# Pairwise products of each row: who issues the stores

## The chip, the cores and the metric

The kernel runs on one core of one Trainium2 chip. The metric is the device time of one execution in microseconds (us); the time of a version is the median of its runs. Beside it stands the span of a profiled execution, which is a little shorter because it leaves out what lies before the first and after the last recorded instruction.

A core has several engines that work side by side, each with its own list of instructions: VectorE (DVE in the profile), ScalarE (ACT), GpSimd (POOL), SyncE (SP) and TensorE (PE, not used here). Data move between the off-chip memory and the on-chip memory through 16 DMA engines. An engine starts such a transfer by an instruction in its own list; the letter q after an engine's name in the profile marks that side of it (SPq).

## The reference

For each of 4096 rows of 256 numbers, all products of two elements of the row are wanted, each pair once: the upper triangle of the outer product, 256 x 257 / 2 = 32896 numbers.

```python
# inputs: r_inputs, 4096 x 256, float32
dot = jnp.einsum('bi,bj->bij', inputs, inputs)
iu, ju = jnp.triu_indices(d)          # d = 256
return dot[:, iu, ju]                 # 4096 x 32896, float32
```

The input has 4.19 MB, the output 538.97 MB. There are two operations in the whole kernel that matter: the multiplication, and the writing of the output.

## The kernel before

Partition p of the on-chip memory holds the rows 32p to 32p + 31. The work is cut into 16 groups of two rows per partition (REPEAT = 2), and each group into 5 pieces of the output's columns (PIECES = 5), so there are 80 tiles. A tile has 128 partitions x 2 rows x up to 6592 columns of float32 and lies in one of three buffers that are used in turn.

```python
P = 128
UNIT = 64
REPEAT = 2
PIECES = 5
BUDGET = 0.95
FIRST = [512, 1536, 3584]
...
    xpool = ctx.enter_context(tc.tile_pool(name="x", bufs=1))
    opool = ctx.enter_context(tc.tile_pool(name="o", bufs=3))

    x_in = x.rearrange("(p r) d -> p (r d)", p=P)
    x_out = out.rearrange("(p g r) c -> g p r c", p=P, r=REPEAT)
```

The whole input is loaded once, in three transfers (of 256, 1792 and 2048 KB) that SyncE issues:

```python
    cuts = [0, REPEAT * d, total // 2, total]
    for a, b in zip(cuts, cuts[1:]):
        nc.sync.dma_start(xt[:, a:b], x_in[:, a:b])
```

Each tile is then computed and stored. ScalarE takes the first runs of columns of a block, VectorE the rest; a run is one element of the row times a stretch of the row. The two rows of a tile are stored by one transfer each (line 139 of the kernel), 128 rows of up to 26368 contiguous bytes. The very first tile is stored in four blocks, so that its first stores can start early.

```python
    for g in range(groups):
        for c, (lo, hi) in enumerate(zip(borders, borders[1:])):
            o = opool.tile([P, REPEAT, slot], F32, tag="o", name=f"o_{g}_{c}")
            first = g == c == 0
            cuts = [lo, *(FIRST if first else []), hi]
            for a, b in zip(cuts, cuts[1:]):
                block = runs(d, a, b)
                k = split(block, 0.0 if first else BUDGET * REPEAT * (b - a))
                for i, j, at, length in block[:k]:
                    ...
                        nc.scalar.activation(...)          # line 123
                ...
                for (i, j, at, length), m in interleave(block[k:]):
                    ...
                    nc.vector.tensor_tensor(...)           # line 132
                for r in range(REPEAT):
                    nc.sync.dma_start(x_out[g][:, r, a:b], o[:, r, a - lo : b - lo])   # line 139
```

That makes 79 x 2 + 4 x 2 = 166 stores. The framework puts in the semaphore waits: a store waits until VectorE and ScalarE have written its block, and the computation of a tile waits until the stores of the tile three back have landed.

Of the kernel before, what the change touches and what calls it, by code (L numbers as in the profile page):

```python
# [1 line left out]

# [4 lines left out]

F32 = mybir.dt.float32
AF = mybir.ActivationFunctionType
ALU = mybir.AluOpType  # L10
# [9 lines that stand above are left out]
def even_borders(lo: int, hi: int, pieces: int) -> list[int]:  # L20
    units = (hi - lo) // UNIT
    return [lo + units * c // pieces * UNIT for c in range(pieces)] + [hi]


def runs(d: int, lo: int, hi: int) -> list:


    found, at = [], 0
    for i in range(d):
        a, b = max(at, lo), min(at + d - i, hi)  # L30
        if a < b:
            found.append((i, i + a - at, a, b - a))
        at += d - i
    return found


def vector_ops(block: list) -> list:

    ops, k = [], 0
    while k < len(block):
        i, j, at, n = block[k]
        m = 2 if k + 2 < len(block) and i == j else 1
        ops.append((block[k], m))
        k += m
    return ops


def interleave(block: list) -> list:


    half = len(block)
    while half and len(vector_ops(block[:half])) > len(vector_ops(block[half:])):
        half -= 1
    a, b = vector_ops(block[:half]), vector_ops(block[half:])
    return [op for k in range(max(len(a), len(b))) for ops in (a, b) for op in ops[k : k + 1]]


def vector_time(block: list) -> float:
    return sum(68 + 1.046 * REPEAT * n * m for (*_, n), m in vector_ops(block))


def split(block: list, budget: float) -> int:


    scalar, k = 0.0, 0
    while k < len(block):
        scalar += REPEAT * (184 + 0.837 * block[k][3])  # L70
        if vector_time(block[k:]) <= budget or scalar > vector_time(block[k + 1 :]):
            break
        k += 1
    return k


def window(ap: bass.AP, free: list) -> bass.AP:
    return bass.AP(ap.tensor, ap.offset, [list(ap.ap[0]), *free])


@with_exitstack
def kernel(
    ctx: ExitStack, tc: tile.TileContext, x: bass.AP, out: bass.AP
):

    nc = tc.nc  # L90
    n, d = x.shape
    width = out.shape[1]
    assert n % (P * REPEAT) == 0 and width == d * (d + 1) // 2 and width % UNIT == 0
    groups = n // (P * REPEAT)
    borders = even_borders(0, width, PIECES)
    slot = max(b - a for a, b in zip(borders, borders[1:]))
# [8 lines that stand above are left out]
    total = n // P * d  # L105
    xt = xpool.tile([P, total + 1], F32, name="x")
    nc.vector.memset(xt[:, total:], 0.0)  # L107
# [14 lines that stand above are left out]
                        row = (g * REPEAT + r) * d  # L122
                        nc.scalar.activation(  # L123
                            o[:, r, at - lo : at - lo + length],
                            xt[:, row + j : row + j + length],
                            AF.Copy,
                            scale=xt[:, row + i : row + i + 1],
                        )
                row = g * REPEAT * d
                for (i, j, at, length), m in interleave(block[k:]):  # L130
                    at -= lo
                    nc.vector.tensor_tensor(  # L132
                        o[:, :, at : at + m * length],
                        window(xt[:, row + j :], [[d, REPEAT], [1, m], [1, length]]),
                        window(xt[:, row + i :], [[d, REPEAT], [1, m], [0, length]]),
                        ALU.mult,
                    )
                for r in range(REPEAT):
                    nc.sync.dma_start(x_out[g][:, r, a:b], o[:, r, a - lo : b - lo])  # L139


# [1 line left out]
_INS = ["r_inputs"]  # L143
_OUTS = [((4096, 32896), "float32")]


# [20 lines left out]
```

## Time and profile before

| what | value |
|---|---|
| time, median of 3 runs | 1274.17 us (1274.16 to 1274.32) |
| span of the profiled execution | 1272.5 us |
| VectorE busy, instructions | 996.1 us, 1813 |
| ScalarE busy, instructions | 486.7 us, 1547 |
| GpSimd busy, instructions | 0.2 us, 4 |
| moved by DMA | 543.43 MB |
| stores of a full row, time from issue to landing | 27.2 us (median of those of 3296 KB) |

How to read it: an engine's busy time is the sum of its instructions' durations; the instructions that only start a transfer or wait are not in it. The page also gives rows of 40 digits, the busy share of 40 equal slices of the span in tenths, and for each DMA queue the number of packets, the megabytes and the share of 16 engines' span that its packets took. A packet is one piece of a transfer on one DMA engine. A line of the timeline gives start, duration, engine, source line, operation, output and input shapes and count, and in brackets how long the engine had been idle before and what ended the idle time.

### The profile page before, as it was taken

The numbers are of one execution on the slowest core, as the hardware profiler recorded it, in microseconds if no ns is written. First come the engines' busy times: TensorE is split into PE (matmuls) and PEld (weight loads), VectorE is DVE, ScalarE is ACT, GpSimd is POOL, SyncE is SP. The second block draws the span as 40 slices with busy tenths as digits, with TensorE's granted clock in tenths as the row PEclk, the third lists the DMA queues.
The fourth block names the chain that finished last, engine by engine and source line by source line (L and its number), as shares of the span: only waits on it lengthen the run. The fifth ranks groups of instructions, "written<-read, shape, count | busy, mean of one in ns | idle before, by whom it ended". The sixth has DMA issues, their size and how long they took to land.

```text
span 1272.5 us, 3975 instructions
## 1 busy us (share of the span) xinstructions
DVE 996.1 (78%) x1813; ACT 486.7 (38%) x1547; POOL 0.2 (0%) x4
## 2 busy tenths in 40 slices
DVE  8987887878777787777877777777777777777770
ACT  5523535234342433424334252342523425234250
POOL 0000000000000000000000000000000000000000
DMA  9999999999999999999999999999999999999998
GB/s 384 435 433 430 434 433 427 434 432 427 431 428 432 429 430 431 429 431 429 433 427 431 429 431 429 431 430 430 429 432 427 433 427 432 428 432 429 431 427 346
DMA packets 24367, 543.43 MB, mean 427 GB/s; under 512 B 2704, under 2 KB 2704, under 8 KB 3344
## 3 DMA queue, kind: packets, MB, share of 16 engines
q1 hardware_dynamic: 24336, 543.17, 99.8%
q14 instruction: 31, 0.25, 0.0%
HBM read 4.19 MB, written 538.97 MB: 427 GB/s over the span
## 4 chain that ended last, share of the span: by engine, by line
DMA 70%; DVE 25%; issue 1%; SPq 1%; DVEq 0%
DMA out_dram<-o 70%; DVE o L132 25%; SPq L139 1%; DMA x<-in_r_inputs_dram 1%; DVEq L132 0%; SPq L110 0%
## 5 line engine op out<-in xcount | busy, mean ns | idle before, releaser
L132 DVE TENSOR_TENSOR o<-x 128x356 f32<-128x356 f32 (+61 forms) x1812 | 996.1, 634 | 239.9 <-DMA out_dram<-o 191.1
L123 ACT ACTIVATE o<-x 128x253 f32<-128x253 f32 (+41 forms) x1546 | 485.4, 404 | 748.6 <-DMA out_dram<-o 732.8
L123 ACT ACT_TABLE_LOAD x1 | 1.3, 1283 | 0.7 <-PEq L154 0.7
L107 DVE MEMSET x<- 128x1 f32 x1 | 0.1, 59 | 0.8 <-PEq L154 0.8
L154 POOL MEMSET const-uint8-127<- 128x1 uint8 x1 | 0.1, 102 | 0.0
L154 POOL MEMSET const-bfloat16-1.0<- 128x1 bf16 x1 | 0.1, 101 | 0.0
L154 POOL MEMSET const-float32-0.0<- 128x1 f32 x1 | 0.1, 98 | 0.2 <-issue 0.2
L154 POOL MEMSET const-float32-1.0<- 128x1 f32 x1 | 0.1, 98 | 0.0
## 6 DMA issues: line engine op xcount, KB each, us to landing
out_dram<-o SPq DMA_DIRECT2D x128, 3296.0 KB, 27.2
out_dram<-o SPq DMA_DIRECT2D x30, 3264.0 KB, 28.9
out_dram<-o SPq DMA_DIRECT2D x2, 1472.0 KB, 13.3
x<-in_r_inputs_dram SPq DMA_DIRECT2D x1, 2048.0 KB, 12.3
out_dram<-o SPq DMA_DIRECT2D x2, 1024.0 KB, 10.0
x<-in_r_inputs_dram SPq DMA_DIRECT2D x1, 1792.0 KB, 6.8
out_dram<-o SPq DMA_DIRECT2D x2, 512.0 KB, 10.2
out_dram<-o SPq DMA_DIRECT2D x2, 256.0 KB, 10.0
```

What stands on the lines that cost most here:

```text
L107: nc.vector.memset(xt[:, total:], 0.0)
L123: nc.scalar.activation(o[:, r, at - lo : at - lo + length], xt[:, row + j : row + j + length], AF.Copy, scale=xt[:, row + i : row + i + 1],)
L132: nc.vector.tensor_tensor(o[:, :, at : at + m * length], window(xt[:, row + j :], [[d, REPEAT], [1, m], [1, length]]), window(xt[:, row + ...
L139: nc.sync.dma_start(x_out[g][:, r, a:b], o[:, r, a - lo : b - lo])
L154: nc = _bacc.Bacc("TRN2", target_bir_lowering=False, num_devices=1)
```

## The change

The stores are issued by GpSimd in place of SyncE. [...] The computation, the tiles, the buffers and the transfers' shapes stay as they are, and so do the three loads, which SyncE still issues. The purpose is to have the stores on an engine that has nothing else to do, with a queue of their own.

```diff
@@ -136,7 +136,7 @@
                         ALU.mult,
                     )
                 for r in range(REPEAT):
-                    nc.sync.dma_start(x_out[g][:, r, a:b], o[:, r, a - lo : b - lo])
+                    nc.gpsimd.dma_start(x_out[g][:, r, a:b], o[:, r, a - lo : b - lo])
```

## The prediction, made before the changed kernel had run

> **What bounds the kernel now.** I read the utilisation rows of the page first, then its DMA queues, then the timeline of the steady part with the idle times in it, then the issues of the stores, and last the records of single DMA packets and landings.
>
> ```profile
> span 1272.5 us, 3975 instructions
> DVE 996.1 (78%) x1813; ACT 486.7 (38%) x1547; POOL 0.2 (0%) x4
> DMA  9999999999999999999999999999999999999998
> GB/s 384 435 433 430 434 433 427 434 432 427 431 428 432 429 430 431 429 431 429 433 427 431 429 431 429 431 430 430 429 432 427 433 427 432 428 432 429 431 427 346
> ...
> q1 hardware_dynamic: 24336, 543.17, 99.8%
> ...
> HBM read 4.19 MB, written 538.97 MB: 427 GB/s over the span
> ```
>
> The DMA row is full in every slice but the last, and the rate is flat at about 430 GB/s. The one queue of the kernel's transfers covers 99.8% of 16 engines' span. VectorE is busy 78% of the time and GpSimd does nothing after four memsets. This is a kernel limited by the transfer of its output.
>
> The timeline of a steady stretch shows how much slack stands behind that:
>
> ```profile
> 611.30 12.48 DVE L132 TENSOR_TENSOR o<-x 128x1008 f32<-128x1008 f32 x13 [3.15 <-DMA out_dram<-o]
> ...
> 626.98 12.37 DVE L132 TENSOR_TENSOR o<-x 128x896 f32<-128x896 f32 x14 [3.20 <-DMA out_dram<-o]
> 642.61 12.42 DVE L132 TENSOR_TENSOR o<-x 128x768 f32<-128x768 f32 x17 [3.26 <-issue]
> ...
> 658.21 12.38 DVE L132 TENSOR_TENSOR o<-x 128x612 f32<-128x612 f32 x21 [3.17 <-DMA out_dram<-o]
> ...
> 673.91 6.35 ACT L123 ACTIVATE o<-x 128x37 f32<-128x37 f32 x23 [9.95 <-DMA out_dram<-o]
> 673.93 6.32 DVE L132 TENSOR_TENSOR o<-x 128x372 f32<-128x372 f32 x19 [3.34 <-DMA out_dram<-o]
> ```
>
> Five tiles begin between 611.30 and 673.93, so one tile takes 62.63 / 4 = 15.66 us. VectorE needs 12.4 us of it and then waits 3.2 us for a buffer. A tile is two DMAs of 3296 KB, 6.75 MB, and 6.75 MB in 15.66 us is 431 GB/s, the rate of the page. There are three buffers. When VectorE starts a tile, the stores of the tile three back have just landed, and two tiles' stores are queued, 2 x 15.66 = 31.3 us of transfer. After 12.4 us, when it issues the new stores, 31.3 - 12.4 = 18.9 us are still ahead of them. The issues of line 139 confirm this:
>
> ```profile
> L139 SPq DMA_DIRECT2D out_dram<-o x166: 332/380/1227, 4.8 to 1237.4; - x166
> ...
> DMA to landing us min/median/max: 9.0/27.1/34.9
> ```
>
> The first store of a pair should land 18.9 + 7.8 = 26.7 us after its issue and the second 18.9 + 15.7 = 34.6 us after; the median is 27.1 and the maximum 34.9. SyncE spends 0.38 us on an issue. So a store may become ready up to about 18.6 us later than now (three buffers give 3 x 15.66 = 47.0 us a round, less 12.4 of VectorE, less 15.7 of its own transfer, less 0.3 of semaphores) before an engine runs dry.
>
> The packet records say what the transfer itself consists of. 24336 packets in 169 DMAs (166 stores and 3 loads) are 144 each, that is 16 engines x (8 rows + 1 semaphore write). A row of 26368 B goes as one packet: 16384 of them have a median of 980 ns, a mean of 983. Shorter ones take 84 ns (2048 B), 159 (4096 B), 309 (8192 B), 611 (16384 B). From the first and third: (8192 - 2048) B / (309 - 84) ns = 27.3 B/ns per engine, and 84 - 75 = 9 ns that every packet costs beside its bytes. Each engine carries 543.17 / 16 = 33.95 MB; at 26368 / 983 = 26.8 B/ns that is 1266 us of pure packets. The span can't be under that, and only about 6.5 us lie on top of it.
>
> Those 6.5 us have a place: in the last DMA 13 engines land between 1265.8 and 1266.8 us on the trace's clock, and three at 1269.7, 1270.7 and 1271.6. The three lags over 1266.8 add up to 2.9 + 3.9 + 4.8 = 11.6 us, and the instruction queue has 37 packets of 8192 B at 312 ns, 11.5 us. I take it (an inference) that the instruction fetches ride on these three engines, and the slowest one sets the end.
>
> [...] The trace of before [...] shows 0.38 us per issue against 7.8 us per transfer, so the issue has nothing to save. [...]
>
> **The change part by part.** In the built programs VectorE and ScalarE run the same instructions in the same order; 166 stores leave SyncE's list and the same 166, same shapes, stand in GpSimd's.
> - Removed: 166 issues x 0.38 us = 63 us of SyncE, all beside transfers. On the path: 0.
> - Added: [...] Each lies under 18.9 us of queued transfers. On the path: 0 in the steady part.
> - Start: the first store is issued at 4.8 us, but loads are being moved until about 14 us (the page has 12.3 us to landing for the third one, issued at about 2). [...] The loads keep SyncE's queue and no longer stand in one line with the stores, so the big third load (needed only from the ninth group) yields some share to them. I count 0, at best -1.5 us: the first 20 us move 353 GB/s, which loses 20 x (1 - 353/430) = 3.6 us, and 1.9 of that is launch.
> - End: the last pair is issued at 1236.9 and ends 34 us later[...]. I allow +0.5 us for GpSimd's closing drain.
> - The packets: the same rows on the same 16 engines. The way of the software descriptors to the engines could cost a few ns for each. I allow 1.5 ns of the 983, or 0.15%, 2 us in all.
> Sum: 1274.2 + 0 + 0 + 0.5 + 2 = 1276.7; against the possible gain at the start I take 0.7 off: 1276 us.
>
> **The rivals.** (a) Rows cut into smaller packets. [...] the trace gives the price: 9 ns a packet. A cut at 4096 B makes 6 x 159 + 75 = 1029 ns of a row in place of 980, +5%, some 1337 us; at 8192 B 3 x 309 + 75 = 1002, +2.2%, 1302 us; at 16384 B 611 + 375 = 986, +0.6%, 1282 us. Against it: the hardware left the 26 KB row whole, so the engines take it. (b) GpSimd as the bound: it needs over 7.8 us a store[...]; at 10 us the whole would be 1660 us. Nothing in the profile speaks for it, nothing measures it either. (c) VectorE keeps GpSimd from writing descriptors for as long as it computes. Even then a set is delayed by no more than a burst of 12.4 us, less than 18.6, and the 3.2 us pause after every tile is just when the stores become ready. 1276 us again; so this rival[...] would not show. (d) One engine of 16 is slower by software descriptors. All engines carry the same bytes and three buffers can't hide a steady lag: 1% of one engine is 12.6 us, 2% gives about 1300. (e) A gain, because the path to the transfer queue gets freer: the 1266 us of packets allow at most 8 us, 0.6%.
>
> **Range and chances.** No rival makes it over 2% faster, since the packets alone forbid it; 0.02 is left for surprises in the packets' own time. For slower by over 2%, above 1299.7 us, I give (a) 0.05, (b) 0.03, (d) and the unknown 0.04: 0.12. The rest is same. The low end, 1270, is the start's gain plus a better spread over the engines; the high end, 1292, is a lag of some 1.3% on one engine, or the 16 KB cut with a smaller lag.
>
> **What would show it right or wrong.** Right: a software queue in place of q1 with 23904 packets (166 x 144) and the same 538.97 MB; packets of 26368 B near 983 ns; VectorE's pauses still 3 us a tile, ended by the stores; the median time to landing near 27 us; DMA at 9 in all slices. (a) would show as several times more packets. (b) as DMA slices below 9 with GpSimd issuing without pause. (c) as longer times from VectorE's last product to the first packet, or longer means of line 132 than 634 ns. (d) as a growing spread between the landings of one DMA, today 0.5 us at the start and 5.8 us at the end.

## The result, and the profile after

| what | before | after |
|---|---|---|
| time, median of 4 runs | 1274.22 us (1274.16 to 1274.32) | 1289.63 us (1289.49 to 1289.88) |
| ratio to before, 95% interval | | 1.0121 (1.0104 to 1.0139) |
| span | 1272.5 us | 1288.1 us |

The changed kernel is 1.2% slower. That lies inside the range of the prediction, but its loss of 15.4 us is far above the 2 us that lie in the predicted 1276 us. These rows of the page answer to the ones shown of before:

```profile
span 1288.1 us, 3975 instructions
...
DVE 995.7 (77%) x1813; ACT 486.7 (38%) x1547; POOL 88.1 (7%) x170
...
DMA  9999999999999999999999999999999999999996
GB/s 389 426 424 425 432 425 427 424 429 427 430 423 426 427 431 426 428 422 430 427 429 424 428 426 430 426 428 423 431 426 428 425 428 425 425 430 424 428 426 266
...
q0 software_dynamic: 23776, 538.98, 98.4%
q1 hardware_dynamic: 432, 4.19, 0.9%
```

The stores have a queue of their own, q0, which the page calls software_dynamic; SyncE's q1 is hardware_dynamic. A store from GpSimd is called a software store below. The computing engines do the same work in the same time. GpSimd has 88 us of issues and is 93% idle. The transfers are still at 9 in every slice but the last, so nothing starves; but the steady rate is 427 GB/s between 100 and 1200 us, where before it was 430, and the last slice is emptier. The pauses of VectorE show that the buffers are still waited for in the same way:

```profile
617.89 12.48 DVE L132 TENSOR_TENSOR o<-x 128x1008 f32<-128x1008 f32 x13 [3.54 <-DMA out_dram<-o]
...
630.92 1.06 POOL L139 DMA_DIRECT2D out_dram<-o  x2 [14.97 <-issue]
...
634.32 12.37 DVE L132 TENSOR_TENSOR o<-x 128x896 f32<-128x896 f32 x14 [3.95 <-DMA out_dram<-o]
...
649.87 12.42 DVE L132 TENSOR_TENSOR o<-x 128x768 f32<-128x768 f32 x17 [3.18 <-DMA out_dram<-o]
...
665.27 12.38 DVE L132 TENSOR_TENSOR o<-x 128x612 f32<-128x612 f32 x21 [2.98 <-DMA out_dram<-o]
...
681.06 9.09 DVE L132 TENSOR_TENSOR o<-x 128x372 f32<-128x372 f32 x30 [3.41 <-DMA out_dram<-o]
```

Five starts from 617.89 to 681.06 make 15.79 us a tile, 0.13 us more than before; all of it is in the pauses. The queue in front of a store is as long as it was. These are the issues of the stores (minimum, median and maximum in ns) and their times to landing:

```profile
L139 POOL DMA_DIRECT2D out_dram<-o x166: 531/533/681, 5.2 to 1250.9; - x166
...
DMA to landing us min/median/max: 8.5/27.5/35.1
```

Where the time went is seen best at the end, when no new work comes. The columns are the stretch, its length, VectorE, ScalarE and GpSimd busy, the TensorE clock, the mean busy share of the 16 DMA engines and the rate. First before, then after:

```profile
1260.00:1264.00 4.00, 0.00 (x0) 0.00 (x0) 0.00 (x0) 1.00 0.98 422
1264.00:1266.00 2.00, 0.00 (x0) 0.00 (x0) 0.00 (x0) 1.00 0.74 316
1266.00:1268.00 2.00, 0.00 (x0) 0.00 (x0) 0.00 (x0) 1.00 0.18 79
1268.00:1270.00 2.00, 0.00 (x0) 0.00 (x0) 0.00 (x0) 1.00 0.15 66
```

```profile
1268.00:1270.00 2.00, 0.00 (x0) 0.00 (x0) 0.00 (x0) 1.00 0.92 396
1270.00:1272.00 2.00, 0.00 (x0) 0.00 (x0) 0.00 (x0) 1.00 0.49 211
1272.00:1274.00 2.00, 0.00 (x0) 0.00 (x0) 0.00 (x0) 1.00 0.49 211
1274.00:1276.00 2.00, 0.00 (x0) 0.00 (x0) 0.00 (x0) 1.00 0.49 211
1276.00:1278.00 2.00, 0.00 (x0) 0.00 (x0) 0.00 (x0) 1.00 0.49 211
1278.00:1280.00 2.00, 0.00 (x0) 0.00 (x0) 0.00 (x0) 1.00 0.52 224
1280.00:1282.00 2.00, 0.00 (x0) 0.00 (x0) 0.00 (x0) 1.00 0.31 132
1282.00:1284.00 2.00, 0.00 (x0) 0.00 (x0) 0.00 (x0) 1.00 0.09 40
```

Before, 13 engines were done by 1266.8 us and three came after. Now the share stands near 0.5 for ten microseconds: half of the engines are done, and the other eight still have some 11 us of their packets to move. The landing records agree: the last store lands on eight engines between 1270.2 and 1271.0 us and on the other eight between 1281.7 and 1284.9. The spread of a store's landings grows evenly over the run, from 1.0 us in the first ten stores to 14.4 in the last ten.

The packet records say when it happens. Packets of a full row (26368 B) have a median of 982 ns, but a mean of 990.6 where it was 983.3; 689 of 16384 took 1040 ns or more, against 41 before. In the steady part (100 to 1200 us) 564 of 615 such packets start within 3 us after the second issue of a tile, most in the second of these microseconds. There are no gaps: over all engines, the packets' durations grow by 9.2 us per engine, and the time until the last landing by 9.5.

The excess of a stretched packet is taken over the median of its size. The packets of full tiles with more than 60 ns of it add up to 113.6 us of engine time, against 11.4 before. The difference of 102.2 us over eight engines would be 12.8 us each; these engines fell behind the others by 10.6 us more than before. The trace does not name a packet's engine, but an engine starts a packet some 4 ns before the one ahead of it ends, so that packets can be strung into chains, and the chain through a store's packets ends with one of the store's 16 landings. (Where two engines change packets in the same nanoseconds, a link is a guess.) Between 200 and 700 us, 310 of the 341 stretched full-row packets stand in chains that end with one of the eight late landings. So the stretched packets and the lag belong together.

So my first theory: something that belongs to a software store takes time from eight of the DMA engines for a moment after each issue, in proportion to its descriptors. By these I count one for each row and one semaphore write for each engine (in the traces the writes are packets of 4 B and 9 ns), 144 for a store of 128 rows; row descriptors are those of the rows alone. The rivals: a fixed cost of each software store; VectorE at work hindering GpSimd; a property of certain DMA engines, whatever memory they serve.

### The profile page after: what moved, and what is told of

It reads as the page before. It is cut to its first block, busy times and chain, and to the rows that moved or that the text cites. A ratio compares the mean times of both kernels' runs of the same rounds, so it can differ in the third digit from the quotient of the medians.

```text
span 1288.1 us, 3975 instructions
## 1 busy us (share of the span) xinstructions
DVE 995.7 (77%) x1813; ACT 486.7 (38%) x1547; POOL 88.1 (7%) x170
## 3 DMA queue, kind: packets, MB, share of 16 engines
q0 software_dynamic: 23776, 538.98, 98.4%
## 4 chain that ended last, share of the span: by engine, by line
DMA 91%; DVE 4%; issue 1%; POOLq 0%; POOL 0%; SPq 0%; DVEq 0%
DMA out_dram<-o 91%; DVE o L132 4%; DMA x<-in_r_inputs_dram 1%; POOL out_dram L139 0%; POOLq L163 0%; SPq L110 0%; DVEq L132 0%; POOLq L139 0%
## 5 line engine op out<-in xcount | busy, mean ns | idle before, releaser
L139 POOL DMA_DIRECT2D out_dram<-o x166 | 87.9, 534 | 1163.1 <-issue 1139.9
## 6 DMA issues: line engine op xcount, KB each, us to landing
out_dram<-o POOLq DMA_DIRECT2D x2, 1472.0 KB, 12.8
```

Source lines behind the costliest of these rows:

```text
L139: nc.gpsimd.dma_start(x_out[g][:, r, a:b], o[:, r, a - lo : b - lo])
```

## The experiments

Each kernel from GpSimd, except pool_332 and mixed, was run beside a twin from SyncE with the same stores. In the tables, the two halves are the eight engines that land the last store first and the next five, on the trace's clock: ranks, since the engines have no names there. The last three also carry instruction fetches and are left out of the halves: strung into chains in the same way, 30 of the 31 fetch packets of before stand in those of the last three landings.

### How much goes with stores, how much with descriptors

Both rows of a tile in one store (sp_both, pool_both; the queue is `nc.sync` in the one and `nc.gpsimd` in the other):

```diff
-                for r in range(REPEAT):
-                    nc.gpsimd.dma_start(x_out[g][:, r, a:b], o[:, r, a - lo : b - lo])
+                nc.gpsimd.dma_start(x_out[g][:, :, a:b], o[:, :, a - lo : b - lo])
```

> Both rows of a tile leave in one store from SyncE: 83 stores of 256 rows in place of 166 of 128, the same rows. It is the reference for pool_both. All theories: the time before, 1274 us, within 2 us, since 83 semaphore writes of 9 ns per engine less are 0.7 us; landing spread at the end near 5.8 us.

> The same 83 stores of 256 rows from GpSimd. The number of row descriptors is that of the changed kernel, the number of stores is half. If the loss goes with the descriptors, the difference to sp_both is about 14.5 us (15.4 x 22576/23904). If it is a fixed cost of each software store, it is about 7.7 us. If it is VectorE that meets GpSimd, it should fall with the number of GpSimd's instructions, to about half as well.

Two stores again, but split by columns, so that each has 256 rows of half the length (sp_halves, pool_halves):

```diff
-                for r in range(REPEAT):
-                    nc.gpsimd.dma_start(x_out[g][:, r, a:b], o[:, r, a - lo : b - lo])
+                mid = (a + b) // 2
+                for s, t in ((a, mid), (mid, b)):
+                    nc.gpsimd.dma_start(x_out[g][:, :, s:t], o[:, :, s - lo : t - lo])
```

> Each tile leaves in two stores, split by columns: 166 stores, each of 256 half rows of some 13 KB, so twice the packets with the bytes and the number of stores as before. All theories: one more packet per row at 9 ns makes 166 x 8 x 9 ns = 12 us, about 1286 us. It is the reference for pool_halves.

> The same 166 stores of 256 half rows from GpSimd: twice the descriptors of the changed kernel with the same number of stores. If the loss goes with the descriptors, the difference to sp_halves is about 29 us (15.4 x 45152/23904). If it is a fixed cost of each software store, it stays at about 15 us. The stretched packets should again stand 1.5 to 3.5 us after a pair of issues, longer or more of them by the first theory.

Four stores a tile, each of 128 half rows (pool_332; the edit is shown against pool_halves; it has no twin of its own and is held against sp_halves, which has the same packets of data and half the stores):

```diff
-                for s, t in ((a, mid), (mid, b)):
-                    nc.gpsimd.dma_start(x_out[g][:, :, s:t], o[:, :, s - lo : t - lo])
+                for r in range(REPEAT):
+                    for s, t in ((a, mid), (mid, b)):
+                        nc.gpsimd.dma_start(x_out[g][:, r, s:t], o[:, r, s - lo : t - lo])
```

> 332 stores from GpSimd, each of 128 half rows: the packets and row descriptors of pool_halves with twice its number of stores. The three pairs so far (8.8 us for 83 stores, 15.4 for 166, 17.9 for 166 with twice the rows) fit 80 ns a store and 2.3 us for each 21248 row descriptors. That gives 332 x 0.080 + 2 x 2.3 = 31 us over sp_halves, about 1321 us. If the loss went with the row descriptors alone, it would stay at pool_halves, 1308 us.

| from GpSimd / from SyncE | stores, row descriptors | times, us | difference | earlier half later by | later half later by | last landing later by |
|---|---|---|---|---|---|---|
| pool_both / sp_both | 83, 21248 | 1283.48 / 1274.73 | 8.8 | 0.7 | 8.7 | 7.7 |
| after / before | 166, 21248 | 1289.63 / 1274.22 | 15.4 | 4.6 | 15.2 | 13.3 |
| pool_halves / sp_halves | 166, 42496 | 1308.26 / 1290.35 | 17.9 | 2.7 | 17.2 | 15.4 |
| pool_332 / sp_halves | 332, 42496 | 1315.26 / 1290.35 | 24.9 | 11.7 | 26.4 | 24.2 |

Ratios to before: pool_both 1.0073 (1.0058 to 1.0088), sp_both 1.0003 (0.9994 to 1.0011), pool_halves 1.0267 (1.0252 to 1.0282), sp_halves 1.0127 (1.0110 to 1.0144), pool_332 1.0322 (1.0305 to 1.0339).

My theory fails in its plain form: twice the descriptors in as many stores cost 2.5 us more (15.4 to 17.9), not 14. A fixed cost of each store comes nearer, 8.8 us where it gives 7.7 and 17.9 where it gives 15, but fails in pool_332: with twice the stores of pool_halves, 24.9 us and not 36. The straight line through the first three pairs, with 31 us for the fourth, was too steep as well (24.9; and of these some 1.5 us, by estimate, are the 166 semaphore writes of 9 ns that sp_halves doesn't have).

The columns of the halves can't be read straight off in the last two rows. A tile is computed only when all 16 engines have stored the tile three back, so a lead that comes near the slack of 18.6 us should leave the leading engines without work. In pool_halves the lead of one half over the other stops growing at 15.0 us from about 1100 us on, in pool_332 at 16.4 from about 900; the landings of one store, with the three engines of the fetches, are then 18 and 19 us apart. From there on the number of engines with a packet in hand falls from 16 to 7 or 8 now and then, in pool_332 from 1114.3 to 1115.6 us for example. The rates of pool_332's 40 slices (32.8 us each) become uneven from the 30th on:

```profile
GB/s 384 423 417 420 419 418 421 420 419 419 419 420 419 419 419 419 420 419 419 420 419 420 419 418 420 418 421 419 420 413 418 413 420 412 419 419 408 421 411 271
```

So the equal leads at the end, 14.5 and 14.7 us, say nothing about stores and rows, and most of the 2.7 and 11.7 us of the earlier half is waiting: at 800 us it was 0.3 and 3.0. Between 100 and 800 us no engine waits, and the lateness of the halves against the twin, taken at the last store of each tile, gives these slopes:

| from GpSimd / from SyncE | stores of a tile | earlier half loses, ns a tile | its lead grows by, ns a tile |
|---|---|---|---|
| pool_both / sp_both | 1 of 256 rows | 7 | 107 |
| after / before | 2 of 128 rows | 53 | 139 |
| pool_halves / sp_halves | 2 of 256 half rows | 5 | 220 |
| pool_332 / sp_halves | 4 of 128 half rows | 57 | 292 |

The lead grows with both: 32 ns for a store and 74 ns for each 256 rows, taken from the first two kernels, give 212 and 276 ns for the other two, within 6%. (It is a fit; nothing tells what the two parts are.) As the expectation of pool_halves has it for the first theory, there are more stretched packets with twice the rows: 526 over 60 ns in these 700 us, where the changed kernel has 387, and 480 of them again start 1 to 3 us after an issue. What all 16 engines lose is another matter. It is small where a store has 256 rows and some 55 ns a tile where it has 128, with two stores and with four. It lies in every packet: the median full row takes 982 ns where it took 980 before, the median half row 500 in pool_332 and 498 in sp_halves, while the medians of pool_both and sp_both (982) and of pool_halves and sp_halves (498) are equal. Why is not shown, and no two rows of the table differ in the number of stores alone: each doubling of the stores also halved the rows of one.

GpSimd itself is far from being the bound. The three issues, of pool_both, pool_halves and pool_332 in this order:

```profile
L138 POOL DMA_DIRECT2D out_dram<-o x83: 717/717/847, 5.2 to 1245.2; - x83
```

```profile
L140 POOL DMA_DIRECT2D out_dram<-o x166: 717/717/847, 4.6 to 1267.8; - x166
```

```profile
L141 POOL DMA_DIRECT2D out_dram<-o x332: 531/531/678, 4.5 to 1280.4; - x166
```

A store of 256 rows takes 717 ns to issue and one of 128 rows 531, whatever the rows' length (as a straight line, 345 ns and 1.45 ns a row), where the transfer of a full row of each partition takes 7.8 us.

### Half of the stores from each engine

```diff
-                for r in range(REPEAT):
-                    nc.gpsimd.dma_start(x_out[g][:, r, a:b], o[:, r, a - lo : b - lo])
+                for r, q in enumerate((nc.sync, nc.gpsimd)):
+                    q.dma_start(x_out[g][:, r, a:b], o[:, r, a - lo : b - lo])
```

> The whole kernel, with the first row of each tile stored from SyncE and the second from GpSimd: 83 software stores in place of 166. If each software store costs its time on the engines, the difference to before is about half, 7 to 8 us; if the lag comes from having a second queue beside the hardware one at all, it isn't halved; if the engines share out two queues unevenly, it may be larger.

1282.52 us, ratio 1.0064 (1.0047 to 1.0081): 8.3 us over before, a little over half of 15.4. The later half of the engines is 6.7 us later than before where it was 15.2, and the earlier half 2.8 us where it was 4.6. Of the 8.3 us, 4.9 lie before the last landing, where they were 13.3 with all stores from GpSimd, and 3.3 after it, in the closing of the program. So half of the software stores bring somewhat less than half of the loss in the transfers, and a second queue beside the first costs nothing of its own that could be seen.

### Without the computation

Three tiles are filled with a constant and stored again and again: the output has the constant in it, and VectorE is idle after the first 42 us, ScalarE from the start. (The pool has one buffer for each of the three tags.)

```diff
+    tiles = [opool.tile([P, REPEAT, slot], F32, tag=f"o{k}", name=f"o_{k}") for k in range(3)]
+    for t in tiles:
+        nc.vector.memset(t[:], 1.0)
     for g in range(groups):
         for c, (lo, hi) in enumerate(zip(borders, borders[1:])):
-            (all computation)
+            o = tiles[(g * PIECES + c) % 3]
+            for r in range(REPEAT):
+                nc.gpsimd.dma_start(x_out[g][0:128, r, lo:hi], o[0:128, r, : hi - lo])
```

> Nothing is computed: three tiles are filled once and 160 stores of 128 rows leave them from SyncE, all of the output. The reference for pool_nocomp: 1266 us of packets and a late start of some 14 us or less, about 1270 to 1285 us.

> The same stores from GpSimd with VectorE and ScalarE idle. If the loss lies between the software descriptors and the transfers alone, the difference to sp_nocomp is 12 to 16 us, as in the changed kernel (15.4). If VectorE's products are needed for it, it is under 3 us.

1272.13 us from SyncE, ratio 0.9984 (0.9977 to 0.9990), and 1289.48 us from GpSimd, 1.0119 (1.0104 to 1.0134): 17.4 us apart with VectorE idle, a little more than the 12 to 16 expected. VectorE is not the cause. The ends of the two, in the columns of above without ScalarE, SyncE's first:

```profile
1266.00:1268.00 2.00, 0.00 (x0) 0.00 (x0) 1.00 1.04 448
1268.00:1270.00 2.00, 0.00 (x0) 0.00 (x0) 1.00 0.00 0
```

```profile
1272.00:1274.00 2.00, 0.00 (x0) 0.00 (x0) 1.00 0.65 277
1274.00:1276.00 2.00, 0.00 (x0) 0.00 (x0) 1.00 0.49 211
1276.00:1278.00 2.00, 0.00 (x0) 0.00 (x0) 1.00 0.49 211
1278.00:1280.00 2.00, 0.00 (x0) 0.00 (x0) 1.00 0.49 211
1280.00:1282.00 2.00, 0.00 (x0) 0.00 (x0) 1.00 0.49 211
1282.00:1284.00 2.00, 0.00 (x0) 0.00 (x0) 1.00 0.49 211
```

From SyncE all 16 engines land the last store within 0.3 us; from GpSimd eight do by 1274.2 us and eight between 1284.6 and 1284.8. Nothing else is left in these programs, so the two halves come from the software stores alone. (The stretched packets lie as before: between 200 and 700 us, 388 of the 395 are in chains of the eight late landings.) The three late engines are gone as well, with 2 packets in the instruction queue of sp_nocomp in place of 31.

### Which memory the stores read

That the loss belongs to the memory of the low partitions was a guess of mine; no run had shown it. As in the kernels without computation, but only the rows of half of the partitions leave; half of the output stays unwritten. (sp_lo and pool_lo take partitions 0 to 63, sp_hi and pool_hi 64 to 127.)

```diff
-                nc.gpsimd.dma_start(x_out[g][0:128, r, lo:hi], o[0:128, r, : hi - lo])
+                nc.gpsimd.dma_start(x_out[g][0:64, r, lo:hi], o[0:64, r, : hi - lo])
```

> Nothing is computed: three tiles are filled once, and of each of the 160 stores of 128 rows only the rows of partitions 0 to 63 leave, from SyncE; half of the output stays unwritten. The reference for pool_lo; [...] the rate should be about half of 430 GB/s and the time some 1250 to 1290 us.

> The same stores of partitions 0 to 63 from GpSimd. If the loss is traffic of the software descriptors[...], the difference to sp_lo is 160 x 60 to 90 ns, 9 to 15 us or more, though nothing is computed. If it belongs to particular DMA engines[...], it is the same here and in pool_hi, and smaller[...]. If VectorE's products cause it, it is under 2 us.

> As sp_lo with partitions 64 to 127: the reference for pool_hi, within 1% of sp_lo.

> The stores of partitions 64 to 127 from GpSimd. If the loss is traffic[...], these rows don't meet it: under 3 us over sp_hi, with all 16 engines landing close together. If it belongs to particular engines or to each software store on all engines, it is as large as in pool_lo.

| partitions | from SyncE | from GpSimd | mean of a full-row packet, SyncE / GpSimd | its 90th percentile |
|---|---|---|---|---|
| 0 to 63 | 1339.56 us | 1340.79 us | 2050.0 / 2051.5 ns | 2062 / 2080 ns |
| 64 to 127 | 1339.54 us | 1338.78 us | 2050.5 / 2048.6 ns | 2062 / 2061 ns |

Ratios to before: 1.0512 (1.0495 to 1.0530), 1.0524 (1.0508 to 1.0539), 1.0512 (1.0497 to 1.0528), 1.0510 (1.0494 to 1.0526), in the order sp_lo, pool_lo, sp_hi, pool_hi.

In size this was a miss: I had expected 9 to 15 us for the low half, and the two halves differ by 2.0 us at most. The SyncE twins are also slower than the 1250 to 1290 us expected of sp_lo, since they move 205 GB/s and not half of 430. But the packets tell them apart. Sorted by the time of a packet's middle after the nearest earlier issue, their mean excess over the median of their size is

```
us after the issue   2.0-2.5  2.5-3.0  3.0-3.5  3.5-4.0  |  5.0-5.5  6.0-6.5
pool_lo, ns             11.8     16.5     15.8     19.6  |    -16.1    -12.3
pool_hi, ns             -1.3     -8.6     -6.1     -2.3  |    -13.8     -8.0
```

From the low partitions the packets are some 20 to 30 ns longer for two microseconds after each issue than at other times; from the high ones no such hump stands out, and the two SyncE twins have none. All of these kernels run on all 16 engines (their DMA share is 1.00), at 205 GB/s. So the hump belongs to the partitions that are read and not to certain engines. What stretches the packets was not shown, nor that the eight late engines of the changed kernel are those that read the low partitions. Why the time of the low half grew so little (1.2 us) I can't say: with half of the partitions a full row's packet takes 2050 ns and not 980, from SyncE as well, the SyncE twin has a spread of 18 us between its engines anyway, and it is narrower from GpSimd (14.0 us in pool_lo, and 16.4 in pool_hi where sp_hi has 19.6), which may hide most of the cost.

## Why the prediction was right or wrong

**What bounds the kernel** was right, and is why the issues themselves moved nothing: 166 issues of 0.38 us were taken from the path's side and 166 of 0.53 us put there, at no gain and no cost.

**The slack of 18.6 us** was right for a store's delay: median landing 27.5 us (27 expected), pauses of 3.0 to 4.0 us, no slice of transfers below 9 until the last. The kernels with half rows later came to its end from another side, by the lead of some engines over others.

**The start** was right: the first store is issued at 5.2 us in place of 4.8, and the first 20 us move 352 GB/s where they moved 353.

**The end** was sized too small: "I allow +0.5 us for GpSimd's closing drain". SyncE is through with its closing waits at 1285.3 us, GpSimd at 1287.4, 2.1 us later; before, the two were 0.03 us apart.

**The packets** are the step that failed: "The way of the software descriptors to the engines could cost a few ns for each. I allow 1.5 ns of the 983, or 0.15%, 2 us in all." The sentence before it, "the same rows on the same 16 engines", took them for alike. The mean grew by 7.3 ns, and the mean isn't what counts. Each engine carries 1264 full rows. The earlier half lost 4.6 us, 3.6 ns a row, the later half 15.2 us, 12.0 ns a row, and the slower half sets the end. I had this mechanism only as rival (d), "One engine of 16 is slower by software descriptors", and there only as a lag of one engine. It was eight, by 0.9% against the others. What follows from it was sized well: 1% for 12.6 us, a spread that grows through the run. So 1289.63 us lies within the range because its high end, 1292, was left for a lag of 1.3%; the sum itself, 1276 us, had no such lag in it. That the lag of eight engines had the size that was reserved for one is luck.

The sum took the choice of the issuing engine for one of the time to start a transfer, 0.38 or 0.53 us. Here it changed the transfers too, by 13.3 us at the last landing.

The new sum closes on the span. The last landing moved from 1271.6 to 1284.9 us, 13.3 us: the 15.2 us of the later half, less 1.9 us because the last of the three engines with instruction fetches now ends 3.1 us behind that half where it was 5.0. From the last landing to the end it is 3.24 us where it was 0.87, which is 2.37 us more. 13.27 + 2.37 = 15.64 us, the difference of the spans.

One reading of the prediction was off: it set 37 packets of the instruction queue, 11.5 us, against the 11.6 us of the three late engines. 31 of them lie within the span, 9.6 us; that they ride on these three engines holds all the same, by the chains of packets.

**The rivals.** (a) did not come. No full row was cut: 16384 packets of 26368 B stand in both traces. Short rows were even put together: the 256 rows of 2048 B of the first two stores appear as 128 packets of 4096 B, which is why the queue has 23776 packets and not 23904. (b) was wrong by a factor of 15: 0.53 us a store against 7.8. (c) could not show in the steady part of the changed kernel, where 137 of the 138 issues between 100 and 1200 us fall into VectorE's pauses. In pool_halves and pool_332 about half of the stores are issued while VectorE multiplies, and these issues take as long as those in the pauses, 717 and 531 ns; the mean of line 132 is 626 ns in the changed kernel, not above 634. So nothing was seen of it. (e) did not come.

**What stays open.** That software stores alone make eight engines late is shown (pool_nocomp). That these are the engines which read the low partitions is a guess from the hump in pool_lo, where it cost 1.2 us over sp_lo, and what stretches the packets there was not shown. The lag goes with the stores and with the rows, by a fit to four kernels. The loss of all 16 engines, 4.6 us in the changed kernel, lies in the packets' durations too (2 ns more in the median of 1264 rows are 2.5 us of it); its cause wasn't tried.

## What to carry to other kernels

Here the transfers were the bound and a store landed 27 us after its issue, so the choice of the issuing engine won nothing by its issue time (0.38 us from SyncE, 0.53 from GpSimd); it still lost 15.4 us through what its stores did to the transfers. For these plain stores SyncE's queue was the better one; where GpSimd must issue, few stores with long rows are what to try first, since 83 stores lost 8.8 us, 166 lost 15.4, or 17.9 with twice the rows, and 332 lost 24.9. With transfers that are spread over all engines, look at the slowest engine and not at the mean (here one half lost 4.6 us and the other 15.2): the busy share at the end of the run and the spread of one transfer's landings show it. When comparing such runs, see whether the lead of the fast engines has come to the end of the buffers: from there on, at a lead of 15.0 us in pool_halves and 16.4 in pool_332, they waited, and the totals no longer added up from their parts.

## What the runs showed that I had not expected

Instruction fetches cost this kernel up to 5 us: they ride on three of the 16 DMA engines, which land the last store up to 5.0 us after the others. Without the computation, with 2 fetch packets, the spread is 0.3 us, and sp_nocomp is 2.1 us faster than before although its first store leaves only when a tile has been filled. Making packets half as long cost sp_halves 16.1 us, where 9 ns a packet gave 12: the median half row takes 498 ns, so two take 14 ns more than the 982 of a full row in sp_both.
